# Four layers of a convolutional block on one core: new buffers, two spills to DRAM, and layers 1 to 3 as passes over small blocks

## The chip, the core and the metric

The kernel runs on one core of one Trainium2 chip. The core has a matrix engine (TensorE, PE in the profile, with its weight loads shown apart as PEld), three engines that work element by element (VectorE or DVE, ScalarE or ACT, GpSimd or POOL), and SyncE (SP), which here only issues DMA transfers. Each engine runs its own list of instructions in order, and they wait for each other through semaphores. Data sits in SBUF, 128 partitions wide; matmuls write to PSUM, whose banks hold 512 f32 values per partition. The metric is the device time of one execution in microseconds; the kernel before takes 4568.75 us as the median of three runs (4568.31 to 4569.31).

## The reference

The input x has 4 images of 256 channels and 64 x 64 positions, N = 4096 positions in all, in f32. Each of four layers computes `x = x + layer(gn(x))`, where `gn` is a group norm over groups of 8 channels.

- Layer 0: a 3x3 convolution of 256 to 256 channels, a group norm (groups of 32) and relu give `xs`. Three 1x1 projections of `xs` to 128 channels give theta, phi and g. `softmax(theta^T phi) g` over all 4096 x 4096 pairs gives y. A 1x1 convolution back to 256 channels, a second group norm, and `w_y * 0.1 + xs` is the layer's result.
- Layer 1: each position's channels are scaled to unit length; a 384x256 matrix gives q, k and v in 4 heads of 32. q is softmaxed over the 32 channels of a head, k over the 4096 positions. `context = k v^T` per head, `out = context^T q`, a 256x128 matrix, and again unit length.
- Layer 2: two small networks (256 to 8 channels, relu, mean over positions) make, for each image, a 3x3 kernel for each channel and a 256x256 matrix. The layer is the depthwise 3x3 convolution and then that matrix.
- Layer 3: the channel means go through a small network and a softmax over 4 experts; the layer is a product with the mixed 256x256 matrix.

## The kernel before

Channels lie on partitions in two halves `h` of 128, positions along the free dimension. `forward` (L33) holds the whole state in a pool of 8 buffers of 128x4096 f32, called slots: the residual `r`, normalised copies (`xn`, `xg`), `xs`, theta, phi, g, the attention's probabilities, q, k, v and qT of layer 1, `dw` of layer 2, and streamed weights (`wp2`, `ex`). For every image it calls `layer0` to `layer3` one after the other.

- `group_stats` (L124) runs `bn_stats` (L130) over 16 pieces of 512 of a finished tensor, joins them (L131), averages over a group with two tiny matmuls against a block matrix (`pm` L133, `pv` L141), and takes a square root on ScalarE (L144) and a reciprocal on VectorE (L145). `normalised` (L160) then writes a whole normalised copy on VectorE (L166).
- In `layer0` the convolution is 18 matmuls (9 taps, 2 channel halves) per 512 output positions into a PSUM tile of 1024 (L286), evicted by ScalarE (L289). Edge rows and columns are cut off by `window`.
- `attention` (L184) takes 512 queries at a time, and runs over 16 blocks `m` of 256 keys: `logits(m+1)` is two matmuls (L196) and one exp of 128x1024 on ScalarE (L198); then two matmuls add to `py` (L206), and VectorE adds the probabilities into `tot` (L211). At the end of the 512 queries, two matmuls of ones with `tot` give the sums `pss` (L214); VectorE takes a reciprocal (L216), two reductions for a range check (L218, L219), and the product with `py`, which overwrites theta (L220). GpSimd adds xs to r meanwhile (L324).
- In `layer1` squares (L359), their sums over channels (`ps_ss` L362, single-column matmuls), qkv (L374), the q softmax with its maximum (L392 to L398), the k maximum over all positions (L408 to L418), the exp of k (L423), the context (L427), the sums of k (L431) and the output loop (L445 to L461) are passes over the whole image.
- In `layer2` the depthwise convolution is done by VectorE in two halves of 32 rows, 9 operations each per channel half (L504, L506), then the 256x256 product (L519) with its residual add (L522).
- In `layer3` the product (L561), the add (L564) and the output DMA, issued by GpSimd (L565).

No order is written out by hand. The program is given to Tile, a planner that puts the instructions of each engine in order when the program is built: of the instructions that are ready by its own estimate of durations, an engine takes the one that stands earliest in the program. It also hands out the buffers of each pool (a tag with a number of buffers) and inserts the waits. So an instruction can stand ahead of others that precede it in the program text, and the engine then keeps to that order whatever the real durations are. The trace shows such cases: statistics of the next image's x stand between the depthwise operations of this one.

After the last image the sums of the softmax are checked against a range; outside it the whole program is run again in another form that subtracts row maxima (`attention_by_rows`). With these inputs it isn't run.

Of the kernel before, what the change touches and what calls it, by code (L numbers as in the profile page):

```python
# [8 lines left out]
F32 = mybir.dt.float32  # L9
# [4 lines left out]
P = 128  # L14
# [11 lines left out]
SUM_MAX, SUM_MIN = 1e30, 1e-25  # L26
# [6 lines left out]
def forward(ctx: ExitStack, tc: tile.TileContext, sums, x, wc, wtpg, ww, wqkv, wout, w1cat, wd2,  # L33
                       bd2, wp2, bp2, experts, rw1, rw2, vec, btp, bg, bo, b1cat, out):

# [6 lines left out]
    slots = ctx.enter_context(tc.tile_pool(name="slots", bufs=9 if sums is None else 8))  # L42
# [6 lines left out]
    def slot(name):  # L49
        return slots.tile([P, N], F32, tag="slot", name=name)  # L50
# [7 lines left out]
    def acc(name):  # L58
        return psa.tile([P, 512], F32, tag="acc", name=name)
# [123 lines left out]

    def attention(b, theta, phi, g):  # L184

        NM = N // CH * 4
        for q in range(NQ):
            cols = bass.ts(q, 512)
            py = acc("ps_y")
            tot = tp.tile([P, CH], F32, tag="tot", name="tot")  # L190
            probs = slot(f"pr_{b}_{q}").rearrange("p (k n) -> p k n", n=CH)

            def logits(m):
                ps = wide("ps_f")
                for s in range(2):
                    nc.tensor.matmul(ps[:, bass.ts(s, 512)], phi[:, bass.ts(2 * m + s, P)], theta[:, cols],  # L196
                                     start=True, stop=True)
                nc.scalar.activation(probs[:, m % 4, :], ps, AF.Exp)  # L198

            logits(0)  # L200
            for m in range(NM):
                if m + 1 < NM:
                    logits(m + 1)
                pr = probs[:, m % 4, :]
                for s in range(2):
                    nc.tensor.matmul(py, g[:, bass.ts(2 * m + s, P)], pr[:, bass.ts(s, 512)],  # L206
                                     start=(m == 0 and s == 0), stop=(m == NM - 1 and s == 1))
                if m == 0:
                    nc.vector.tensor_copy(tot, pr)
                else:  # L210
                    nc.vector.tensor_tensor(tot, tot, pr, ALU.add)  # L211
            pss = bank("ps_sum")
            for s in range(2):
                nc.tensor.matmul(pss, ones, tot[:, bass.ts(s, 512)], start=(s == 0), stop=(s == 1))  # L214
            inv = tp.tile([P, 512], F32, tag="inv", name="inv", bufs=1)
            nc.vector.reciprocal(inv, pss)  # L216
            at = b * NQ + q
            nc.vector.tensor_reduce(sums[:, 0, at:at + 1], pss, AX.X, ALU.max)  # L218
            nc.vector.tensor_reduce(sums[:, 1, at:at + 1], pss, AX.X, ALU.min)  # L219
            nc.vector.tensor_tensor(theta[:, cols], py, inv, ALU.mult)  # L220

    def attention_by_rows(b, theta, phi, g):
# [48 lines left out]
    def layer0(b, r):  # L271
# [54 lines left out]
        if sums is None:  # L326
            attention_by_rows(b, theta, phi, g)
        else:
            attention(b, theta, phi, g)
# [247 lines left out]
def conv_preact_kernel(ctx: ExitStack, tc: tile.TileContext, *args):  # L577
# [3 lines left out]
    sums = gp.tile([P, 2, B * NQ], F32, name="sums")  # L581
    forward(tc, sums, *args)

    ext = gp.tile([P, 2], F32, name="ext")
    nc.vector.tensor_reduce(ext[:, 0:1], sums[:, 0, :], AX.X, ALU.max)
    nc.vector.tensor_reduce(ext[:, 1:2], sums[:, 1, :], AX.X, ALU.min)
    nc.vector.tensor_scalar(ext[:, 0:1], ext[:, 0:1], SUM_MAX, None, ALU.is_le)
# [4 lines left out]
    with tc.If(in_range < 1):  # L594
        forward(tc, None, *args)
# [58 lines left out]
```

## Time and profile before

| | |
|---|---|
| median of 3 runs | 4568.75 us (4568.31 to 4569.31) |
| the profiled execution: its own time, its span | 4574.75 us, 4573.0 us |
| mean granted TensorE clock | 0.905 |
| TensorE busy | 3885.9 us, 85% of the span |
| VectorE busy | 1932.7 us, 42% |
| ScalarE busy | 934.0 us, 20% |
| GpSimd busy | 92.4 us, 2% |
| DMA | 51.90 MB, 11 GB/s over the span |

The span runs from the first instruction to the last. A row of a group of instructions gives the line, the engine, the operation, the tiles written and read, the shape and the count, then busy time and mean duration. TensorE's records need care: one f32 matmul is two records, a busy TensorE isn't TensorE at its peak, and its clock is granted in steps that the profile shows (1.00 is full). Idle time of an engine that isn't the bound costs nothing.

### The profile page before, as it was taken

To read this page: it belongs to the slowest core of one execution; us is meant where nothing else is said; L and a number is where in the kernel's file an instruction comes from. 1 tells how busy PE (TensorE), PEld (TensorE's weight loads), DVE (VectorE), ACT (ScalarE), POOL (GpSimd) and SP (SyncE) were. 2 spreads that over 40 slices of the span, in tenths; PEclk is the share of its full clock that TensorE was granted. 3 is DMA by queue.
4 is the path that set the end of the run, shared out by engine and by line. 5 is a ranking of instruction groups with operands and counts; after the bars stand their busy time and mean duration, and the time that the engine had idled before them with its cause. 6 is when DMAs were issued, how large, how long until landed. Compare 5 with 4: busy or idle time off the path is not lost.

```text
span 4573.0 us, 25690 instructions
## 1 busy us (share of the span) xinstructions
PE 3885.9 (85%) x10388; PEld 1917.5 (42%) x10388; DVE 1932.7 (42%) x2154; ACT 934.0 (20%) x1324; POOL 92.4 (2%) x71
## 2 busy tenths in 40 slices
PE   8999998764999999875499999987459999997845
PEld 3444443541444444353244444435324444443622
DVE  1014444569101444556810244454781024445477
ACT  0022223220002222322000222232100022223210
POOL 0010000000001000000000100000000010000000
PEclk9999999676999999967799999997779999998777
DMA  1000000000000000000100000000010000000000
GB/s 72 0 0 0 1 0 0 19 19 34 30 0 0 0 0 0 0 19 19 44 21 0 0 0 1 0 0 19 19 53 12 0 0 0 0 0 0 19 9 38
DMA packets 10318, 51.90 MB, mean 11 GB/s; under 512 B 1744, under 2 KB 2512, under 8 KB 6992
## 3 DMA queue, kind: packets, MB, share of 16 engines
q1 hardware_dynamic: 5584, 33.41, 2.0%
q0 software_dynamic: 4608, 16.78, 0.9%
q8 instruction: 83, 1.36, 0.1%
q14 instruction: 43, 0.35, 0.0%
HBM read 33.40 MB, written 16.78 MB: 11 GB/s over the span
## 4 chain that ended last, share of the span: by engine, by line
PE 66%; issue 19%; DVE 13%; ACT 1%; DMA 0%; POOL 0%; SPq 0%; POOLq 0%; ACTq 0%; DVEq 0%
PE ps_conv L286 21%; PE ps_f L196 14%; PE ps_y L206 14%; DVE dw L506 5%; PE ps_qkv L374 3%; DVE st L130 2%; PE ps_tp L305 2%; PE ps_ex L561 2%; PE ps_ss L362 2%; PE ps_h L474 1%; PE ps_g L315 1%; PE ps_wy L337 1%; PE ps_sum L214 1%; PE ps_pw L519 1%; DVE z L455 1%
## 5 line engine op out<-in xcount | busy, mean ns | idle before, releaser
L211 DVE TENSOR_TENSOR tot<-tot,pr 128x1024 f32<-128x1024 f32 x480 | 588.3, 1226 | 959.5 <-ACT pr L198 956.3
L286 PE MATMUL ps_conv<-xn,wc_s 128*128 128x504 f32 (+3 forms) x2304 | 978.0, 588 | 9.1 <-DVE xn L166 9.1
L196 PE MATMUL ps_f<-theta,phi 128*128 128x512 f32 x2048 | 957.1, 592 | 0.0
L206 PE MATMUL ps_y<-pr,g 128*128 128x512 f32 x2048 | 957.1, 592 | 0.0
L198 ACT ACTIVATE pr<-ps_f 128x1024 f32<-128x1024 f32 x512 | 524.3, 1024 | 1290.4 <-PE ps_f L196 1290.4
L286 PEld LDWEIGHTS ps_conv<-xn,wc_s 128*128 128x128 f32 x2304 | 440.2, 191 | 544.4 <-issue 538.3
L206 PEld LDWEIGHTS ps_y<-pr,g 128*128 128x128 f32 x2048 | 389.1, 190 | 489.8 <-issue 474.2
L196 PEld LDWEIGHTS ps_f<-theta,phi 128*128 128x128 f32 x2048 | 388.8, 190 | 487.9 <-issue 486.0
L130 DVE BATCH_NORM_STATS2 st<-xs 128x6 f32<-128x512 f32 x64 | 41.2, 685 | 930.3 <-ACT xs L289 930.3
L519 PE MATMUL ps_pw<-dw,pk 128*128 128x512 f32 x256 | 131.1, 671 | 265.7 <-DVE pk L512 208.0
L506 DVE SCALAR_TENSOR_TENSOR dw<-xn,dk,dw 128x2016 f32<-128x2016 f32 (+3 forms) x128 | 286.4, 2295 | 0.0
L289 ACT ACTIVATE xs<-ps_conv,vec_s 128x1024 f32<-128x1024 f32 x32 | 35.6, 1114 | 954.3 <-PE ps_conv L286 954.3
L374 PE MATMUL ps_qkv<-wqkv_s,xg 128*128 128x384 f32 x512 | 204.1, 557 | 18.1 <-DVE k L378 9.5
L519 PEld LDWEIGHTS ps_pw<-dw,pk 128*128 128x128 f32 x256 | 54.0, 217 | 339.9 <-DVE pk L512 208.4
L130 DVE BATCH_NORM_STATS2 st<-x 128x6 f32<-128x512 f32 x256 | 160.9, 675 | 5.9 <-DMA x<-in_x_dram 5.7
L216 DVE RECIPROCAL inv<-ps_sum 128x512 f32<-128x512 f32 x32 | 107.4, 3357 | 91.8 <-PE ps_sum L214 91.8
L133 PE MATMUL pm<-mv,avg 128*128 128x2 f32 x48 | 12.2, 323 | 156.9 <-DVE mv L131 156.9
L144 ACT ACTIVATE rstd<-rstd 128x2 f32<-128x2 f32 x24 | 4.9, 204 | 684.7 <-DVE rstd L143 684.7
L561 PE MATMUL ps_ex<-xn,wm 128*128 128x512 f32 x256 | 117.7, 623 | 30.6 <-DVE wm L553 30.6
L374 PEld LDWEIGHTS ps_qkv<-wqkv_s,xg 128*128 128x128 f32 x512 | 106.2, 216 | 85.2 <-issue 18.7
L305 PE MATMUL ps_tp<-xs,wtpg_s 128*128 128x512 f32 x256 | 123.1, 637 | 10.4 <-ACT xs L296 10.4
L362 PEld LDWEIGHTS ps_ss<-ones,sq 128*128 128x128 f32 x512 | 108.3, 313 | 16.0 <-issue 11.2
(145 smaller groups left out, 2316.1 us busy)
## 6 DMA issues: line engine op xcount, KB each, us to landing
x<-in_x_dram SPq DMA_DIRECT2D x16, 1024.0 KB, 7.0
out_dram<-x POOLq DMA_DIRECT2D x32, 512.0 KB, 2.9
wp<-in_wp_dram SPq DMA_DIRECT2D x4, 2048.0 KB, 7.7
ex<-in_experts_dram SPq DMA_DIRECT2D x4, 1024.0 KB, 4.7
wc_s<-in_wc_dram SPq DMA_DIRECT2D x1, 2304.0 KB, 15.9
wtpg_s<-in_wtpg_dram SPq DMA_DIRECT2D x1, 384.0 KB, 15.9
wqkv_s<-in_wqkv_dram SPq DMA_DIRECT2D x1, 384.0 KB, 13.1
bp_s<-in_bp_dram SPq DMA_DIRECT2D x1, 256.0 KB, 2.8
```

The costliest lines, as they stand in the source:

```text
L130: nc.vector.bn_stats(st[:, h, c, :], src[h][:, bass.ts(c, 512)])
L196: nc.tensor.matmul(ps[:, bass.ts(s, 512)], phi[:, bass.ts(2 * m + s, P)], theta[:, cols], start=True, stop=True)
L198: nc.scalar.activation(probs[:, m % 4, :], ps, AF.Exp)
L206: nc.tensor.matmul(py, g[:, bass.ts(2 * m + s, P)], pr[:, bass.ts(s, 512)], start=(m == 0 and s == 0), stop=(m == NM - 1 and s == 1))
L211: nc.vector.tensor_tensor(tot, tot, pr, ALU.add)
L286: nc.tensor.matmul(dst[:, oy, ox], wc_s[:, h, 3 * ty + tx, bass.ts(oh, P)], image(xn[h])[:, iy, ix], start=(k == 0), stop=(k == 17))
L305: nc.tensor.matmul(ps[:, bass.ts(s, 512)], wtpg_s[:, h, k, :], xs[h][:, bass.ts(2 * c + s, 512)], start=(h == 0), stop=(h == NH - 1))
L362: nc.tensor.matmul(pss[:, 4 * c + j:4 * c + j + 1], sq[:, h, bass.ts(j, P)], ones[:, 0:1], start=(h == 0), stop=(h == NH - 1))
L374: nc.tensor.matmul(ps[:, s, 0:3 * HID], xg[h][:, bass.ts(2 * j2 + s, P)], wqkv_s[:, h, :], start=(h == 0), stop=(h == NH - 1))
L506: nc.vector.scalar_tensor_tensor(dst[:, oy, ox], src, dk[:, t:t + 1], dst[:, oy, ox], ALU.mult, ALU.add)
L519: nc.tensor.matmul(ps[:, bass.ts(s, 512)], pk[:, h, bass.ts(oh, P)], dw[h][:, bass.ts(2 * c + s, 512)], start=(h == 0), stop=(h == NH - 1))
L561: nc.tensor.matmul(ps[:, bass.ts(s, 512)], wm[:, h, bass.ts(oh, P)], xg[h][:, bass.ts(2 * c + s, 512)], start=(h == 0), stop=(h == NH - 1))
```

## The change

`forward` is replaced by `conv_preact_fast`; the old form lives on only as the fallback behind the range check (`conv_preact_general`). The new one does the following.

- Fixed buffers instead of slots: `xp` holds the normalised input with a row of zeros above and below each channel half, `big` (128 x 2 x 4096) holds the convolution's output and later the residual stream, `tpg` holds theta, phi and g. Working tiles are small: seven of 128x1024 (`k4`), five of 128x512 (`k2`). PSUM: three banks under one tag (`bank`), three `pf` for the logits, two `acc` for `py` and the sums.
- x is normalised in place, one channel half on VectorE, the other on ScalarE. The convolution writes one bank per 512 positions, with statistics taken right after each eviction.
- After norm and relu, `xs` is written to DRAM (`xs_d`). The attention's result is written to DRAM per 512 queries (`y_d`). Both are read back in `nonlocal_out`, with x itself, which is loaded a second time.
- In attention, exp runs on pieces of 512, three `pr` buffers replace a slot, the two halves of `tot` are added by VectorE before one sum matmul, and the range check's second value comes from a ScalarE pass over the reciprocal (`junk`).
- The statistics that the next norm needs are taken inside the pass that makes the data. The norms are not applied as separate copies in front of layers 2's small network and layer 3's product, but folded into the weights (`w1n`, `wm`, with `b1n`, `b3`).
- Layer 1 runs over eight blocks of 512 positions. It takes no maxima in its softmaxes; the sum of k comes from a column of ones beside v (`v1`), accumulated with the context in `pctx`.
- Reciprocal square roots are taken on GpSimd with `pow` instead of a ScalarE square root and a VectorE reciprocal.
- The depthwise convolution runs in four pieces of 16 rows, its centre tap on ScalarE.
- All output is issued by SyncE.

```diff
+    def k4(name):
+        return wk.tile([P, CH], F32, tag="k4", name=name, bufs=7)
+    def k2(name):
+        return wk.tile([P, 512], F32, tag="k2", name=name, bufs=5)
+    def bank(name):
+        return pp.tile([P, 512], F32, tag="bank", name=name, bufs=3)
+    xp = cp.tile([P, NH, HW + 2, HW], F32, name="xp")
+    big = cp.tile([P, NH, N], F32, name="big")
+    tpg = cp.tile([P, 3, N], F32, name="tpg")
...
+    def rsqrt(o, v):
+        nc.gpsimd.tensor_tensor(o, v, half[:, 0:v.shape[1]], ALU.pow)
...
+    def attend(b):
...
+            def logits(m):
+                pr = wk.tile([P, CH], F32, tag="pr", name="pr", bufs=3)
+                for s in range(2):
+                    pf = pp.tile([P, 512], F32, tag="pf", name="pf", bufs=3)
+                    nc.tensor.matmul(pf, phi[:, bass.ts(2 * m + s, P)], theta[:, cols], start=True, stop=True)
+                    nc.scalar.activation(pr[:, bass.ts(s, 512)], pf, AF.Exp)
+                probs[m] = pr
...
+            nc.vector.scalar_tensor_tensor(inv, tot[:, 0:512], 1.0, tot[:, 512:CH], ALU.mult, ALU.add,
+                                           accum_out=guard[:, 0, at:at + 1])
+            pss = pp.tile([P, 512], F32, tag="acc", name="pss", bufs=2)
+            nc.tensor.matmul(pss, ones, inv, start=True, stop=True)
+            nc.vector.reciprocal(inv, pss)
+            junk = k2("junk")
+            nc.scalar.activation(junk, inv, AF.Copy, accum_out=guard[:, 1, at:at + 1])
+            yt = k2("yt")
+            tt(yt, py, inv, ALU.mult)
+            nc.sync.dma_start(out=y_d[b, :, cols], in_=yt)
+    def nonlocal_out(b):
...
+        for c in range(N // CH):
+            cols = bass.ts(c, CH)
+            for h in range(NH):
+                xs, xr = k4("xs"), k4("xr")
+                nc.sync.dma_start(out=xs, in_=xs_d[b, h, :, cols])
+                nc.sync.dma_start(out=xr, in_=x[b, bass.ts(h, P), cols])
+                stt(xs, big[:, h, cols], sc[:, h:h + 1], xs, ALU.mult, ALU.add)
+                stt(big[:, h, cols], xs, sh[:, h:h + 1], xr, ALU.add, ALU.add)
+                for s in range(2):
+                    nc.vector.bn_stats(st[:, h, 2 * c + s, :], big[:, h, bass.ts(2 * c + s, 512)])
...
+    def linear_attention(b, st):
...
+        pctx = bank("ps_ctx")
+        for c in range(N // 512):
...
+            sq = k4("sq").rearrange("p (h n) -> p h n", h=NH)
+            nc.scalar.activation(sq, xg, AF.Square)
+            s2 = k2("s2")
+            tt(s2, sq[:, 0, :], sq[:, 1, :], ALU.add)
+            ps = bank("ps_ss")
+            for j in range(4):
+                nc.tensor.matmul(ps[:, j:j + 1], s2[:, bass.ts(j, P)], ones[:, 0:1], start=True, stop=True)
...
+            rsqrt(rinv, rinv)
...
+            for j in range(4):
+                ps = bank("ps_qkv")
...
+                nc.scalar.activation(qk[:, j, :], ps[:, 0:2 * HID], AF.Exp, scale=rinv[:, j:j + 1])
+                nc.scalar.activation(v1[:, j, 0:P], ps[:, 2 * HID:3 * HID], AF.Copy, scale=rinv[:, j:j + 1])
...
+            pt = bank("ps_qt")
...
+            for j in range(4):
+                nc.tensor.matmul(pctx[:, 0:P + 1], qk[:, j, HID:2 * HID], v1[:, j, :],
+                                 start=(c == 0 and j == 0), stop=(c == N // 512 - 1 and j == 3))
...
+    def generated(b, st):
...
+        for j in range(R):
+            w = k2("wp2")
+            nc.sync.dma_start(out=w, in_=wp2[:, j, :])
+            stt(pk, w, pb[:, R + j:R + j + 1], pk, ALU.mult, ALU.add)
...
+    def tail(b):
+        mixed(b, generated(b, linear_attention(b, nonlocal_out(b))))
+    for b in range(B):
+        if b > 0:
+            load_x(b)
+        convolve(b)
+        project()
+        attend(b)
+        tail(b)
```

## The prediction

> **What bounds the kernel now.** I read the page first: its busy line, then the slices, then the chain.
>
> ```profile
> span 4573.0 us, 25690 instructions
> PE 3885.9 (85%) x10388; PEld 1917.5 (42%) x10388; DVE 1932.7 (42%) x2154; ACT 934.0 (20%) x1324; POOL 92.4 (2%) x71
> PE   8999998764999999875499999987459999997845
> PEclk9999999676999999967799999997779999998777
> ```
>
> The four images are four equal periods. TensorE is full for two thirds of each and thin in the last third, where the granted clock falls as well. So I cut the second image into its stages with busy times by stretch (columns: PE, PEld, DVE, ACT, POOL, each with its count, then granted clock, DMA share and GB/s):
>
> ```profile
> 1165.00:1409.00 244.00, 243.76 (x576) 110.00 (x576) 13.24 (x19) 7.80 (x7) 0.00 (x0) 0.99 0.00 0
> 1409.00:1416.00 7.00, 1.01 (x5) 0.59 (x4) 3.11 (x12) 2.22 (x3) 0.00 (x0) 0.88 0.00 0
> 1416.00:1461.00 45.00, 44.61 (x193) 27.69 (x194) 9.00 (x8) 13.88 (x13) 18.56 (x8) 0.94 0.00 0
> 1461.00:1914.00 453.00, 453.00 (x1057) 200.63 (x1056) 188.66 (x157) 131.07 (x128) 0.00 (x0) 1.00 0.00 0
> 1914.00:1961.00 47.00, 18.01 (x45) 9.06 (x44) 40.83 (x68) 20.93 (x21) 0.00 (x0) 0.67 0.00 0
> 1961.00:2076.00 115.00, 97.66 (x418) 74.67 (x419) 47.32 (x67) 31.98 (x64) 0.00 (x0) 0.74 0.05 19
> 2076.00:2129.00 53.00, 28.53 (x133) 22.01 (x133) 43.99 (x74) 16.11 (x74) 0.00 (x0) 0.85 0.11 40
> 2129.00:2150.00 21.00, 16.95 (x34) 3.50 (x33) 6.46 (x13) 6.17 (x16) 0.00 (x0) 0.83 0.00 1
> 2150.00:2267.00 117.00, 34.74 (x74) 15.29 (x74) 116.77 (x106) 3.12 (x5) 0.00 (x0) 0.65 0.07 27
> 2267.00:2301.00 34.00, 30.13 (x68) 13.54 (x68) 12.76 (x18) 0.20 (x1) 4.30 (x8) 0.94 0.30 124
> ```
>
> These are: convolution; its norm; projections; attention; output projection with two norms; layer 1 up to its context; layer 1's output; layer 2's hidden layer; depthwise, pointwise and layer 3's gate; layer 3's product. Convolution, projections and attention are TensorE-bound at full clock, 742 of 1136 us. The other third is bound by VectorE (depthwise) or by serial steps on small pieces. Only there can a rewrite of layers 1 to 3 gain.
>
> **The change, per image.** Matmul counts below are pairs of records: one f32 matmul of 512 columns is two records of 0.43 us, 0.86 us.
>
> *Convolution, +2.5 us.* Border rows are now zero rows that are multiplied. The edge forms (441 and 448 columns, 192 records over four images) become 504 and 512: 3040 more columns per image at 512 in 0.43 us. Evictions of 512 on ScalarE and statistics on VectorE lie under 7.7 us of matmul each (uncovered, 16 x 1.25 = 20 us). The norm after it loses a 1.12 us eviction of 1024 for 0.6, one of two last statistics (0.65), sqrt and reciprocal (0.2 each), and gains a `pow` on GpSimd and three small VectorE steps: 0.
>
> **The unknown p.** No row has that `pow` on 128x2 or 128x4. POOL's nearest rows are a 128x128 select, 0.29 us, and a 128x1024 two-operand operation, 2.35 us. The size is nearest the first, the operation heavier, so I take p = 1.0 and keep 0.3 to 2.4. It cannot be below nothing, but the 0.4 us of sqrt and reciprocal it replaces are counted as gone. About eight lie on each image's path.
>
> *Attention, -6.9 us.* The two sum matmuls become one, after a VectorE add of the halves: 0.86 us less, eight times. By the timeline of a query block's end:
>
> ```profile
> 429.28 1.22 DVE L211 TENSOR_TENSOR tot<-tot,pr 128x1024 f32<-128x1024 f32 x1 [2.21 <-ACT pr L198]
> 431.45 1.88 PE L214 MATMUL ps_sum<-tot,ones 128*128 128x512 f32 x4
> 433.17 3.60 PE L196 MATMUL ps_f<-theta,phi 128*128 128x512 f32 x8
> 433.37 3.36 DVE L216 RECIPROCAL inv<-ps_sum 128x512 f32<-128x512 f32 x1 [2.87 <-PE ps_sum L214]
> ```
>
> The last add ends 0.9 us before the sum starts, so the new 0.75 us add still fits. The next block's logits cover the reciprocal: two pairs take 3.44 us, then the first `py` needs an accumulator bank, freed by the reciprocal 3.4 us after the sum. That is the new edge; three `pr` buffers let a third pair run. Exp in halves costs ScalarE 2 x 0.6 us per 3.44 us. Uncovered, the danger is ScalarE's queue (first rival).
>
> *Output projection to layer 1, +7.* After the last sum: 16 matmuls 13.75 us. They cover the last y trip: reciprocal 3.36, product 0.68, write and read about 2.9 each (the nearest rows are 512 KB written in 2.9 and 256 KB read in 2.8), under 11 us in all. Then eviction 0.6, statistics 0.65, group norm 3.6 with p, shift and affine 1.2: 5.8. Then VectorE alone: 8 x (two scalar_tensor_tensor of 1024 at 1.25, by 512 in 0.75 and 2016 in 2.3; two statistics at 0.61) = 29.8. Then group norm 3.6, ScalarE's first normalisation 0.6, hand-overs 0.6. Sum 54 for 47. Before, ScalarE shared the add, GpSimd had added x under attention, and statistics cost 16 x 0.61.
> The 16 reloads of 512 KB sit under those 29.8 if two land per 3.7 us. These rows give 2.9 us for 512 KB and 1.5 MB more in 4.8, so 3.2 us for two; seven buffers are filled during attention.
>
> ```profile
> out_dram<-x POOLq DMA_DIRECT2D x32, 512.0 KB, 2.9
> wp<-in_wp_dram SPq DMA_DIRECT2D x4, 2048.0 KB, 7.7
> ```
>
> The Trainium skill ("DMA: Bandwidth & Descriptors", section Bandwidth) speaks against this: batch to at least 1 MiB, about 2 us being fixed per transfer. Taken as serial, its fit would price 16 loads at some 51 us and this stage 20 us dearer; I go by the rows, since the transfers overlap.
>
> *Layer 1 to its context, -25.* Before, normalise, squares, sums, qkv, two softmaxes, context and key sums follow each other; 7.0 us is one k maximum, and 256 single-column sum records run at clock 0.50. The change drops both maxima, halves the sums, folds key sums into context, and runs eight blocks. In one block TensorE has sums 1.4, eight matmuls of 384 columns 5.4 (0.34 a record), four transposes 0.5, context 1.2: 8.5 us. ScalarE has 2 x 0.62 + 1.06 + 4 x (0.42 + 0.36) + 0.6 = 6.0, VectorE 2.5. `pctx` holds one of three banks; on two, a block's end is exp, sum 0.66, reciprocal 0.25, product 0.68, transposes, copy 0.6, while the next block's sums use the other. That leaves TensorE some 0.9 us idle: 9.4 us, or 9.9 at clock 0.95. First block 9.3, seven more 69, drain and w2 6: 84 for 115; I take 90 for unevenness, with 85 to 130.
>
> *Layer 1's output, 0.* VectorE per block: 2 x 0.68 + 0.15 + 1.22 + 2 x (0.74 + 0.61) = 5.4, so 44, plus 8 to start: 52 for 53. Statistics move in here from layer 2.
>
> *Layers 2 and 3, -3.5.* The hidden layer loses the normalisation ahead of it, but ScalarE now has 8 x 0.87 + 8 x 1.23 = 16.8 us: 19.8 for 21.5 with the centre tap. Depthwise: 64 operations of 1.18 (75.5; before 32 of 2.21 and four centres), pk 5.3, pointwise adds 16 x 0.70, statistics 16 x 0.61, less 1.3 of pk in a wait: 100.5. Last pointwise 3.2, group norm 3.6, gate and mix 6.7: 114 for 117. Layer 3's 29 us stay; pm of the next image can have a bank only after ps_ex: 5.7 us for 4.6.
>
> *DMA issue, 0.* SyncE issues 73 transfers per image for 6: 4 of x, 8 of xs, 16 of y, 16 reloads, 9 of layer 2's weights in pieces, 4 of the experts, 16 of output; GpSimd issues none of the output's 8. At 0.33 to 0.5 us an issue that is some 30 us of its queue, spread over 1136. The next x is issued when depthwise has left its buffer, some 19 us ahead of layer 3's product, and lands (7.0 us for 1 MB, four at once) under the gate and that product's 29 us; if not, up to 11 us more per image. Weight pieces come through five buffers, under depthwise.
>
> Sum: 2.5 - 6.9 + 7 - 25 + 0 - 3.5 = -26 per image, -104. The profiled execution took 4574.75 us (span 4573.0 and 1.75 around it), 6.0 above the median of 4568.75. So 4471 on its scale, **4466** as a median.
>
> On layer 1 the clock matters most. Its row: granted 0.74 there now, 0.50 under single-column sums though TensorE shows busy. The Trainium skill ("TensorE: Matmul & The Clock Gate", Part 1) says half rate comes after an idle window of about 3.4 us. By that rule a block with 0.9 us of idle would stay warm, at 9.4; if 1.4 us sums counted as idle, still no window is empty.
>
> **Rivals.**
> 1. *ScalarE's queue blocks at each query block's end.* `junk` reads the reciprocal. If it stands ahead of the next block's exps, these start 3.4 + 0.6 us after the sum; three `pf` banks hold 2.6 us of logits: 2.25 us stall, 32 times, +72: 4538. For: the planner writes the order by its own estimates, and it put a 7.08 us reduction between two steps of the q softmax. Against: TensorE has no gap at any of 32 ends before.
> 2. *Layer 1's blocks do not overlap* (slower). One block in series: 1.24 + 1.06 + 0.7 + 1.4 + 0.2 + p + 4.7 evictions + 1.7 softmax + 0.5 + 0.6 + hand-overs 0.5 = 13.6, at clock 0.74 about 15.6: 125 + 9 for my 90, +44 per image: 4642. For: `bank` is shared with `pctx`, and buffers seem given out in program order (the next image's loads waited for layer 1's end). Against: before, qkv already ran between the sums. It decides from 90 + 26 = 116 us, so from 9.9 + 26/8 = 13.1 us a block.
> 3. *`pow` is slow* (slower). Beyond the rows, p = 5 costs 8 x 4 = 32 per image: 4594. It decides at 1 + 26/8 = 4.3 us.
> 4. *The spill shows.* If pairs of reloads take 6 us, 48 for 29.8: +18 per image, 4538.
> 5. *The change does little:* gains and losses inside 0.2% (9 us, about what can be told from no change).
>
> ```profile
> 898.16 7.08 DVE L408 TENSOR_REDUCE km<-k 128x128 f32<-128x4096 f32 x1
> 905.15 1.22 DVE L393 TENSOR_TENSOR q<-q,qred 128x1024 f32<-128x1024 f32 x1
> ```
>
> **How the numbers follow.** Forecast 0.42; rivals 0.20, 0.18, 0.08, 0.10; little change 0.02. Low end: layer 1 at 85 and p at 0.3, (5 + 5.6) x 4 = 42 off: 4424. High end takes in rival 2, 4642; a blocked and cold version beyond it is left out. Faster: nearly all of the forecast, three quarters of rivals 1 and 4: 0.63. Slower: rivals 2 and 3, and the ends of 1 and 4: 0.31. Same 0.06. The forecast alone spans 4424 to 4515.
>
> **What would show it.** Attention at about 446 us per image without TensorE gaps; the stretch from last sum to first qkv near 54 with VectorE solid; layer 1's blocks every 9 to 10 us at clock over 0.9; POOL `pow` rows of about 1 us; clock and VectorE of the depthwise stretch as before. I am wrong if the blocks go beyond 13 us, if ScalarE waits for a reciprocal between blocks, or if VectorE waits for reloads.

## The result and the profile after

The changed kernel takes 4725.65 us (median of 4 runs, 4723.11 to 4727.16) against 4569.03 us for the kernel before, measured beside it: a ratio of 1.0342, 95% interval 1.0324 to 1.036. It is 3.4% slower, where the forecast said 2.2% faster; the time lies 84 us above the range's upper end. The profiled execution took 4723.11 us.

The page of the kernel after, its span, busy line of TensorE, and two rows of the 40 slices:

```profile
span 4721.1 us, 26366 instructions
...
PE 3917.5 (83%) x9858; PEld 1887.4 (40%) x9858; DVE 1785.5 (38%) x2202; ACT 1137.2 (24%) x2107; POOL 84.3 (2%) x131
...
PE   7999997745999999675599999967459999996745
...
PEclk9999998767999999876799999977679999997767
```

TensorE has fewer matmul records than before (9858 for 10388) and yet 32 us more busy time: some of the same work ran at a lower clock (granted 0.892 on average, for 0.905 before). The four thin stretches are still there, and they are longer.

The second image cut into the same stages as in the prediction (columns as there: stretch and length, PE, PEld, DVE, ACT, POOL with counts, granted clock, DMA share, GB/s):

```profile
1201.00:1449.00 248.00, 247.53 (x576) 110.33 (x576) 11.92 (x17) 12.03 (x18) 0.00 (x0) 0.99 0.00 0
1449.00:1455.00 6.00, 0.71 (x4) 0.59 (x4) 2.54 (x12) 1.17 (x2) 0.69 (x1) 0.76 0.00 0
1455.00:1500.00 45.00, 43.95 (x193) 27.34 (x194) 4.84 (x7) 18.90 (x24) 0.00 (x0) 0.96 0.48 175
1500.00:1946.00 446.00, 446.00 (x1042) 197.51 (x1041) 181.66 (x151) 156.35 (x270) 0.00 (x0) 1.00 0.01 5
1946.00:2011.00 65.00, 19.28 (x48) 9.54 (x46) 48.11 (x73) 12.46 (x21) 1.45 (x3) 0.64 0.33 106
2011.00:2116.00 105.00, 87.10 (x287) 57.03 (x286) 18.76 (x41) 43.54 (x95) 8.45 (x15) 0.76 0.00 0
2116.00:2199.00 83.00, 41.81 (x137) 33.05 (x138) 44.91 (x73) 14.81 (x66) 8.75 (x9) 0.64 0.00 0
2199.00:2219.00 20.00, 16.21 (x36) 3.43 (x33) 1.49 (x8) 15.63 (x26) 0.00 (x0) 0.90 0.19 55
2219.00:2338.00 119.00, 44.27 (x75) 17.61 (x76) 116.60 (x142) 7.70 (x9) 0.70 (x1) 0.68 0.16 55
2338.00:2375.00 37.00, 33.17 (x76) 15.51 (x76) 14.27 (x26) 1.11 (x1) 0.70 (x1) 0.87 0.29 114
```

Beside the forecast, in us per image (the last column is the run both_bank_edits, told below: the same text with two bank edits):

| stage | before | forecast | after | both_bank_edits |
|---|---|---|---|---|
| convolution, norm, projections | 296 | 298.5 | 299 | 299.3 |
| attention | 453 | 446.1 | 446 | 446.5 |
| last sum to first qkv | 47 | 54 | 65 | 61.2 |
| layer 1, first pass (qkv to ps_o) | 115 | 90 | 105 | 72.3 |
| layer 1, output pass (ps_o to ps_h) | 53 | 52 | 83 | 54.0 |
| hidden layer | 21 | 19.8 | 20 | 20.1 |
| depthwise to gate | 117 | 114 | 119 | 119.3 |
| layer 3's product, next norm | 34 | 34.7 | 37 | 36.9 |

In the kernel before the first qkv stands at 1959.04, two us ahead of the cut that the prediction made; counted from it, 47 and 115 are 45 and 117.

Four images times the differences from the forecast (11 + 15 + 31 + 5 + 2, some 64) are 256 of the 260 us by which the forecast missed. Half of it is in the output pass, which was forecast at no change.

Rows from the timeline of the output pass, weight loads left out (start, length, engine, line, work; in brackets the idle time before and what ended it):

```profile
2124.26 1.97 PE L403 MATMUL ps_zt<-ident,z 128*128 128x128 f32 x8 [4.27 <-DVE z L56]
2126.01 2.86 PE L391 MATMUL ps_o<-w,xp 128*128 128x256 f32 x8
...
2128.12 1.48 DVE L56 TENSOR_TENSOR z<-ps_o,bo_s 128x512 f32<-128x512 f32 x2
2128.89 0.42 ACT L396 ACTIVATE junk<-z 128x256 f32<-128x256 f32 x1 [7.24 <-DVE z L56]
...
2130.89 1.01 POOL L125 TENSOR_TENSOR zr<-zr,half 128x4 f32<-128x4 f32 x1 [7.95 <-DVE zr L397]
2131.93 1.22 DVE L56 TENSOR_TENSOR z<-z,zr 128x1024 f32<-128x1024 f32 x1 [1.12 <-POOL zr L125]
2133.30 1.94 PE L403 MATMUL ps_zt<-ident,z 128*128 128x128 f32 x8 [4.42 <-DVE z L56]
...
2135.03 3.46 PE L391 MATMUL ps_o<-w,xp 128*128 128x256 f32 x8
```

Each block goes through every engine before the next begins: ps_o, add, squares, pow, product, transposes, 9.0 to 9.9 us a block. On TensorE the next block's ps_o stands behind this block's ps_zt, although it needs nothing of it. TensorE idles 4.3 to 4.9 us a block, and the clock goes to 0.64. Before, four blocks of ps_o (32 records) ran ahead of the first transposes, and the pass took 53 us:

```profile
2075.65 9.28 PE L445 MATMUL ps_o<-w,qT 128*128 128x256 f32 x32 [0.58 <-DVE w L440]
2086.38 1.09 PE L459 MATMUL ps_zt<-ident,z 128*128 128x128 f32 x8 [1.45 <-DVE z L455]
```

The first pass of the kernel after, TensorE alone (the last row ends with the window):

```profile
2063.83 8.44 PE L352 MATMUL ps_qkv<-wqkv_s,xg 128*128 128x384 f32 x16 [0.33 <-DVE rinv L343]
2072.11 0.83 PE L368 MATMUL ps_ctx<-v,qk 128*128 128x129 f32 x6
2073.37 0.49 PE L368 MATMUL ps_ctx<-v,qk 128*128 128x129 f32 x2 [0.43 <-ACT v L355]
2075.18 0.63 PE L364 MATMUL ps_qt<-ident,qk 128*128 128x128 f32 x4 [1.31 <-DVE qk L56]
2075.64 0.95 PE L341 MATMUL ps_ss<-ones,s 128*128 128x1 f32 x8
2076.92 3.48 PE L352 MATMUL ps_qkv<-wqkv_s,xg 128*128 128x384 f32 x5 [0.33 <-DVE rinv L343]
```

A block is 12.7 to 13.1 us here, the first one 14.0. The next block's sums and qkv stand behind this block's ps_qt, which waits for the q softmax; the qkv matmuls themselves take 7.0 to 8.4 us (8.4 in the block shown) where the forecast had 5.4.

### The profile page after: what moved, and what is told of

It reads as the page before. It is cut to its first block, busy times and chain, and to the rows that moved or that the text cites. A ratio compares the mean times of both kernels' runs of the same rounds, so it can differ in the third digit from the quotient of the medians.

```text
span 4721.1 us, 26366 instructions
## 1 busy us (share of the span) xinstructions
PE 3917.5 (83%) x9858; PEld 1887.4 (40%) x9858; DVE 1785.5 (38%) x2202; ACT 1137.2 (24%) x2107; POOL 84.3 (2%) x131
## 3 DMA queue, kind: packets, MB, share of 16 engines
q8 instruction: 80, 1.31, 0.1%
## 5 line engine op out<-in xcount | busy, mean ns | idle before, releaser
L231 PE MATMUL ps_conv<-xp,wc_s 128*128 128x504 f32 (+1 forms) x2304 | 990.7, 594 | 10.3 <-DVE xp L203 10.3
L268 PE MATMUL pf<-tpg 128*128 128x512 f32 x2048 | 957.1, 592 | 0.0
L278 PE MATMUL py<-pr,tpg 128*128 128x512 f32 x2048 | 957.1, 592 | 0.0
L269 ACT ACTIVATE pr<-pf 128x512 f32<-128x512 f32 x1024 | 607.9, 596 | 1143.2 <-PE pf L268 1143.2
L231 PEld LDWEIGHTS ps_conv<-xp,wc_s 128*128 128x128 f32 x2304 | 441.6, 192 | 556.4 <-issue 543.7
L278 PEld LDWEIGHTS py<-pr,tpg 128*128 128x128 f32 x2048 | 389.1, 190 | 489.8 <-issue 483.1
L268 PEld LDWEIGHTS pf<-tpg 128*128 128x128 f32 x2048 | 388.8, 190 | 487.9 <-issue 481.2
L59 DVE SCALAR_TENSOR_TENSOR dw<-xp,dk,dw 128x1008 f32<-128x1008 f32 (+1 forms) x256 | 309.6, 1260 | 5.0 <-ACT dw L462 4.9
L246 PE MATMUL ps_tp<-big,wtpg_s 128*128 128x512 f32 x256 | 123.4, 628 | 15.1 <-ACT big L216 12.0
L527 PE MATMUL ps_ex<-big,wm 128*128 128x512 f32 x256 | 124.8, 649 | 0.0
```

The costliest lines, as they stand in the source:

```text
L59: nc.vector.scalar_tensor_tensor(o, a, s, b, op0, op1)
L231: nc.tensor.matmul(dst[:, :, x0:x1], wc_s[:, h, 3 * ty + tx, bass.ts(oh, P)], xp[:, h, c * RB + ty:c * RB + ty + RB, x0 + dx:x1 + dx], sta ...
L246: nc.tensor.matmul(ps, wtpg_s[:, h, k, :], big[:, h, cols], start=(h == 0), stop=(h == NH - 1))
L268: nc.tensor.matmul(pf, phi[:, bass.ts(2 * m + s, P)], theta[:, cols], start=True, stop=True)
L269: nc.scalar.activation(pr[:, bass.ts(s, 512)], pf, AF.Exp)
L527: nc.tensor.matmul(ps[oh], wm[:, h, bass.ts(oh, P)], big[:, h, cols], start=(h == 0), stop=(h == NH - 1))
```

## The experiments

**Theory.** The planner gives a tag's buffers out in the order of the program text, when it places the instruction that first writes them. ps_o of block c+1 and ps_zt of block c share the tag `bank`; ps_zt comes first in the text, so ps_o of the next block gets no bank until this block's last stage has been placed, though a bank stands free. In the first pass ps_ss and ps_qkv of block c+1 wait for ps_qt of block c in the same way. **Rivals:** three banks are too few whatever the order; the cold clock stretches a chain that would otherwise fit; and, for the stretch after attention, y's trip through DRAM.

**1. own_banks_out.** ps_o moves to the three `pf` banks, which are idle after attention (`pf_bank` and `acc_bank` are helpers that take a tile of the tag `pf` or `acc`).

```
-                ps = bank("ps_o").rearrange("p (j o) -> p j o", j=2)
+                ps = pf_bank("ps_o").rearrange("p (j o) -> p j o", j=2)
```

> Edit: the changed kernel, with layer 1's output pass taking its ps_o tiles from the three pf banks, which are idle there, instead of from the bank tag that ps_zt uses as well. No work is added or left out. Theory B (banks): a tag's banks are handed out in the order of the program's first uses, so ps_o of the next block can't get one until ps_zt of this block is placed, and the blocks run one after the other (9.5 us a block, 83 us for the pass). With its own banks the pass is bound by VectorE's 5.4 us a block: about 55 us, 27 us less per image, 4725 - 108 = 4617. Theory W (work): the pass is slow for what was put into it, statistics 1.28 and pow with its hand-overs 1.3 us a block, and for the half clock of its matmuls; then it stays within 3 us of 83, and the time within 4713 to 4738.

Measured: 4615.19 us, ratio to before 1.0098 (1.0081 to 1.0115), 110.5 us less than the kernel after. The output pass by windows (columns as above, here and in what follows):

```profile
2089.20:2143.90 54.70, 32.52 (x137) 25.76 (x138) 42.28 (x73) 14.28 (x65) 8.75 (x9) 0.72 0.00 1
```

From 82.7 to 54.7 us, as expected. VectorE, which the forecast had as the bound, is now busy for 42 of 55 us. This changes both the order of hand-out and the number of banks; experiments 5 and 6 part the two.

**2. own_banks_ctx.** ps_ss goes to the `acc` banks, ps_qt and the context to `pf`; qkv keeps the three of `bank`.

```
-        pctx = bank("ps_ctx")
+        pctx = pf_bank("ps_ctx")
...
-            ps = bank("ps_ss")
+            ps = acc_bank("ps_ss")
...
-            pt = bank("ps_qt")
+            pt = pf_bank("ps_qt")
```

> Edit: the changed kernel, with layer 1's first pass taking ps_ss from the two acc banks and ps_qt and pctx from the three pf banks; ps_qkv keeps the bank tag. No work is added or left out. Theory B: the blocks run every 12.9 us now since ps_ss of the next block must wait for ps_qt of this one, which stands behind the q softmax; TensorE thins out to clock 0.77. With own banks qkv of the next block fills that time: 9.5 to 10 us a block, clock over 0.9, 105 us become about 82, 23 us less per image, 4725 - 92 = 4633. Theory W: ScalarE's order (normalisation, squares and exps of two blocks in one queue) or the pow holds the blocks; then under 5 us per image, 4705 or more.

Measured: 4575.73 us, ratio 1.0013 (1.0004 to 1.0023), 149.9 less than after. The first pass by windows:

```profile
1972.70:2044.80 72.10, 65.16 (x291) 42.10 (x291) 20.00 (x42) 44.40 (x96) 8.43 (x15) 0.97 0.00 1
```

72.1 us for 104.7, ten better than expected: TensorE is busy for 65 of 72 us, with 0.7 us of idle time left in a block of 8.4, and the clock is 0.97 where it was 0.76. The stretch ahead of it fell too, from 65.2 to 61.3, since the first qkv no longer stands behind ps_ss; with it the two stretches together went from 169.9 to 133.4. The forecast's 9.9 us a block was too dear; the cost of sharing was larger than the measured 105 against 90 had made it look.

**3. y_in_sbuf.** y overwrites theta, which the query block no longer needs, and never goes to DRAM.

```
-            yt = k2("yt")
-            tt(yt, py, inv, ALU.mult)
-            nc.sync.dma_start(out=y_d[b, :, cols], in_=yt)
+            tt(theta[:, cols], py, inv, ALU.mult)
...
-            yt = k2("yt")
-            nc.sync.dma_start(out=yt, in_=y_d[b, :, cols])
...
-                nc.tensor.matmul(ps, ww_s[:, bass.ts(h, P)], yt, start=True, stop=True)
+                nc.tensor.matmul(ps, ww_s[:, bass.ts(h, P)], theta[:, cols], start=True, stop=True)
```

> Edit: the changed kernel without the spill of y: the attention's result overwrites theta, as before the change, and the output projection reads it there. Theory S (spill on the path): all but one of the eight reads of y stand behind the last write of y in SyncE's queue, and that write waits for the last reciprocal; TensorE waits 5.9 us and starts the rest late. Without the spill the output projection follows the last sum without a gap: 6 to 8 us less per image, 4725 - 28 = 4697. Rival: the wait only moves, since the last piece needs the reciprocal anyway, and the group norm's end is set by it: under 2 us per image, 4717 or more.

Measured: 4682.63 us, ratio 1.0245 (1.0228 to 1.0262), 43.0 less than after: 8.1 us of it per image in the stretch from the last sum to the first qkv (57.1 for 65.2), the rest in the passes behind it. What it removed, in the timeline of the kernel after (SPq is SyncE's list of DMA issues; the last row ends with the window):

```profile
1946.33 1.88 PE L306 MATMUL ps_wy<-yt,ww_s 128*128 128x512 f32 x4
...
1949.92 0.69 DVE L56 TENSOR_TENSOR yt<-py,inv 128x512 f32<-128x512 f32 x1
...
1950.64 0.32 SPq L294 DMA_DIRECT2D y_d<-yt  x1
1951.12 8.60 SPq L303 DMA_DIRECT2D yt<-y_d  x7
...
1954.13 6.10 PE L306 MATMUL ps_wy<-yt,ww_s 128*128 128x512 f32 x10 [5.93 <-DMA yt<-y_d]
```

Seven of the eight reads are issued behind the last write, although six of them fetch pieces that were written long before. So only one pair of matmuls could start at once, and 5.93 us of TensorE were lost. Why the planner put the six there was not tried.

**4. before_shared_banks.** The other way round: the kernel before, with its ps_zt taken from the tag that ps_o uses.

```
-                pt = bank("ps_zt")
+                pt = wide("ps_zt")[:, 0:512]
```

> Edit: the kernel before, with ps_zt of layer 1's output loop taken from the wide tag that ps_o uses, two buffers for both. No work is added or left out, no pow, no statistics in the loop. Theory B: the same hand-out in program order now serialises the blocks here too: from 5.1 to about 9 us a block, 53 us become 75 to 85, 4569 + 4 x 25 = 4669 (4655 to 4700). Theory W: the loop stays at 53 us within 4, since its work is what it was: 4553 to 4585.

Measured: 4719.1 us, ratio 1.0327 (1.031 to 1.0344). The one line costs the kernel before 150 us, nearly as much as the whole change did. Its output pass by windows:

```profile
2107.90:2198.30 90.40, 43.44 (x133) 32.77 (x134) 47.63 (x74) 16.76 (x74) 0.00 (x0) 0.65 0.06 23
```

90.4 us where before had 53.2, clock 0.65 for 0.85; 37.2 x 4 is the 150 us. The expectation was right in kind and a third too small (150 us more than before, for 100; the time is above its band of 4655 to 4700). Two buffers now serve both stages, so this run alone doesn't part order from number; 5 and 6 do.

**5. one_ring_six_banks.** The text unchanged; `bank` and `pf` become one tag of six.

```
-        return pp.tile([P, 512], F32, tag="bank", name=name, bufs=3)
+        return pp.tile([P, 512], F32, tag="bank", name=name, bufs=6)
...
-                    pf = pp.tile([P, 512], F32, tag="pf", name="pf", bufs=3)
+                    pf = bank("pf")
```

> The kernel after with the pf tag dissolved: all tiles of the bank and pf tags take turns in one ring of six banks, text and order of the program as they are. If banks are too few, six instead of three free the next block: the output pass falls to 55 us or less, the first pass of layer 1 below 90 too, the time to 4615 or below. If it is the order in which a tag's banks are handed out (a bank for the next block's ps_o isn't given before this block's ps_zt has its own), six banks change nothing there: the output pass stays at 80 to 85 us an image, the whole at 4710 to 4735.

Measured: 4704.52 us (4699.48 to 4712.57), ratio 1.029 (1.0274 to 1.0305). The first pass and the output pass by windows:

```profile
2011.20:2112.40 101.20, 85.47 (x285) 55.47 (x285) 18.75 (x41) 43.70 (x95) 8.43 (x15) 0.77 0.00 0
2112.40:2195.20 82.80, 41.70 (x135) 32.94 (x135) 44.95 (x73) 14.61 (x65) 8.74 (x9) 0.66 0.00 0
```

Twice the banks change the output pass by nothing (82.8 for 82.7) and the first pass by 3.5 us. It is not their number. (The time came out 5 us below the expected band.)

**6. front_written_first.** Three shared banks as in the kernel after; only the text is turned, so that ps_o and the adds of the next block stand ahead of this block's squares and transposes.

```
-        for c in range(N // 512):
-            cols = bass.ts(c, 512)
+        def front(c):
             z = k4("z").rearrange("p (j o) -> p j o", j=4)
...
+            return z
+
+        zn = front(0)
+        for c in range(N // 512):
+            cols = bass.ts(c, 512)
+            z = zn
+            if c + 1 < N // 512:
+                zn = front(c + 1)
             zr = sp.tile([P, 4], F32, name="zr", bufs=3)
```

> The kernel after with its three shared banks, but the output loop written so that the ps_o matmuls and the adds of bo of block c+1 stand ahead of the squares and transposes of block c. No bank is added. If the order of hand-out is the cause, the blocks overlap again: output pass 54 to 58 us instead of 83, the whole at 4610 to 4630, as with banks of its own. If three banks are too few for the overlap, it stays above 70 us and 4680.

Measured: 4629.04 us, ratio 1.0128 (1.0112 to 1.0143). The output pass by windows:

```profile
2095.40:2152.90 57.50, 35.47 (x137) 28.37 (x138) 42.23 (x73) 14.11 (x65) 8.75 (x9) 0.71 0.00 1
```

57.5 us without one bank more. With 5, this settles the output pass: the order of hand-out, not the number. It could not be the planner's preference for earlier text alone either, since in experiment 1 the text was as in the kernel after and only the tag differed. That a buffer is given out at its first write, and not at another point, is part of the theory that no run tried.

**7. warm_fill.** Two 128x512 matmuls more a block, into a bank that nobody reads, in TensorE's idle time.

```
+            for s in range(2):
+                wm = pp.tile([P, 512], F32, tag="pf", name="wm", bufs=3)
+                nc.tensor.matmul(wm, ident, z.rearrange("p j o -> p (j o)")[:, bass.ts(s, 512)], start=True, stop=True)
             zr = sp.tile([P, 4], F32, name="zr", bufs=3)
```

> The kernel after with two matmuls of 128x512 more a block in the output pass, which read z after the adds, write a pf bank that nobody reads, and fall into the 4.4 us in which TensorE waits for z. They prolong no other engine's work. If a cold clock is a good part of the 83 us, the granted clock of this window rises from 0.64 to 0.8 or more, the block's own matmuls (3.6 + 1.9 + 1.9 us cold) shrink by a quarter or more, and the pass falls to 70 to 76 us, the whole to 4690 to 4705. If the serial chain through VectorE, ScalarE and GpSimd is all of it, the pass stays at 82 to 86 us and the whole at 4720 to 4740.

Measured: 4699.56 us, ratio 1.0282 (1.0266 to 1.0298), 26 us less with more work done. The output pass by windows, and the groups of its matmuls (count, then busy us and mean ns of one record):

```profile
2113.70:2189.60 75.90, 48.42 (x167) 31.10 (x168) 43.91 (x73) 14.26 (x65) 8.75 (x9) 0.84 0.00 1
```

```profile
L391 PE MATMUL ps_o<-w,xp 128*128 128x256 f32 x256 | 85.5, 494 | 1.9 <-ACT w L382 1.9
...
L395 PE MATMUL wm<-z,ident 128*128 128x512 f32 x128 | 66.6, 644 | 13.9 <-DVE z L56 13.6
...
L406 PE MATMUL ps_zt<-ident,z 128*128 128x128 f32 x256 | 43.2, 323 | 76.4 <-DVE z L56 76.4
```

In the kernel after these records took 584 and 423 ns. The clock rose from 0.64 to 0.84 and the pass fell by 6.8 us, of the 28 that the overlap gives. So the lower clock is about a quarter of the loss, as far as this filling removes it. The overlapped passes of 1 and 6 take 54.7 and 57.5 us at a clock of only 0.71 to 0.72: it is the overlap that makes them short, not the clock.

**8. both_bank_edits.** Experiments 1 and 2 together, y still through DRAM.

```
-        pctx = bank("ps_ctx")
+        pctx = pf_bank("ps_ctx")
...
-            ps = bank("ps_ss")
+            ps = acc_bank("ps_ss")
...
-            pt = bank("ps_qt")
+            pt = pf_bank("ps_qt")
...
-                ps = bank("ps_o").rearrange("p (j o) -> p j o", j=2)
+                ps = pf_bank("ps_o").rearrange("p (j o) -> p j o", j=2)
```

> The change as made, y through DRAM as it is, with the two bank edits only (ps_o in the pf banks; ps_ss, ps_qt and ps_ctx in acc and pf banks). If the hand-out of banks is the one step of the forecast that failed, what is left is the forecast: 4725.65 less 110.5 and 149.9 is 4465, with the 13.6 us by which the three edits together fell short of their sum 4479; qkv to ps_o about 72 us, output pass 52 to 55. If something else took a good part of the difference, it stays above 4510.

Measured: 4461.46 us (4460.4 to 4464.07), ratio 0.9765 (0.9751 to 0.9778). Where the forecast had 4466. Its stages are the table's last column; the two passes of layer 1 by windows:

```profile
1947.00:2019.30 72.30, 65.29 (x292) 42.15 (x292) 20.00 (x42) 44.53 (x97) 8.45 (x15) 0.97 0.00 1
2019.30:2073.30 54.00, 31.44 (x137) 24.90 (x138) 42.30 (x73) 14.76 (x66) 8.76 (x9) 0.72 0.00 1
```

In sum the change does gain what was forecast; the assignment of banks took 264 us, more than all of it.

**9. all_three_mended.** The four lines of both_bank_edits and y over theta.

```
-                ps = bank("ps_o").rearrange("p (j o) -> p j o", j=2)
+                ps = pf_bank("ps_o").rearrange("p (j o) -> p j o", j=2)
...
-            tt(yt, py, inv, ALU.mult)
-            nc.sync.dma_start(out=y_d[b, :, cols], in_=yt)
+            tt(theta[:, cols], py, inv, ALU.mult)
```

> All three edits in one kernel: the output pass's ps_o in the pf banks, ps_ss, ps_qt and ps_ctx in acc and pf banks, y written over theta instead of to DRAM. If the three costs are separate, their gains add: 4725.65 less 110.5, 149.9 and 43.0 is 4422, a period of image 1 of about 1099, and faster than the kernel before by about 3 %. If they share a cost (one and the same cold clock, or the shortage of banks that only moves on), the gains overlap and the time stays between 4450 and 4530.

Measured: 4435.63 us (4435.19 to 4435.94), ratio 0.9705 (0.9692 to 0.9718): the fastest kernel of this study. The two bank edits add up (264.2 for 260.4 as a sum). The time lies between the two bands of the expectation (4422, and 4450 to 4530). y kept in SBUF adds 25.8 here and not 43.0: the stretch after the last sum falls by 8.0 us an image as it did alone (61.2 to 53.2), some 32 in all. Alone, the two passes behind it gained another 10 us over the four images; here they lost 2 (the first pass takes 73.2 us on average for 72.7). (The two profiled executions differ by 28.2 us, the medians by 25.8.) In the kernel after these passes ran at a clock of 0.76 and 0.64; that this is the reason was not tried by itself.

**10. both_passes_by_order.** No more banks; beside 6, the first pass takes normalisation, squares and sums of the next block ahead of this block's qkv and softmax.

```
-        for c in range(N // 512):
+        def front(c):
...
             rsqrt(rinv, rinv)
+            return xg, rinv

+        nxt = front(0)
+        for c in range(N // 512):
+            cols = bass.ts(c, 512)
+            xg, rinv = nxt
+            if c + 1 < N // 512:
+                nxt = front(c + 1)
             qk = k4("qk").rearrange("p (j o) -> p j o", j=4)
```

> No bank more than in the kernel after; the text of both passes of layer 1 is put in another order: the output loop as in front_written_first, and in the first pass the normalisation, squares and ps_ss of block c+1 ahead of the qkv, softmax and ps_qt of block c. Order theory: in the first pass the next block's sums and their pow no longer lie behind this block's transposes, so a block takes 9.5 to 10.5 us and not 12.9, the pass 80 to 88 us, the whole 4629 less 4 x (17 to 25): 4530 to 4561. If the first pass is short of banks (pctx holds one of three), it stays at 100 us or more and the whole at 4610 to 4630.

Measured: 4602.29 us, ratio 1.0073 (1.0058 to 1.0088), a miss: the first pass went from 104.7 to 99.4 us only, while the stretch ahead of it grew by 2.7. The run falls into neither band of the expectation (its second one, for a lack of banks, began at 100 us and 4610), but is next to the second. The pass by windows:

```profile
1985.30:2084.70 99.40, 82.15 (x276) 53.36 (x276) 18.01 (x39) 41.48 (x92) 7.42 (x14) 0.79 0.00 0
```

But in this text ps_qt of block c still stands ahead of ps_qkv of block c+1, so TensorE still has nothing to do during the softmax. The last two runs part that from the number of banks.

**11. softmax_written_last.** As 10, with the front carried on through qkv: the q softmax, ps_qt and ps_ctx of block c stand behind qkv of block c+1. Three banks.

```
-        for c in range(N // 512):
+        def front(c):
...
                 nc.scalar.activation(v1[:, j, 0:P], ps[:, 2 * HID:3 * HID], AF.Copy, scale=rinv[:, j:j + 1])
+            return qk, v1

+        nxt = front(0)
+        for c in range(N // 512):
+            cols = bass.ts(c, 512)
+            qk, v1 = nxt
+            if c + 1 < N // 512:
+                nxt = front(c + 1)
             q = qk[:, :, 0:HID].rearrange("p j (g d) -> p j g d", d=HD)
```

> Three shared banks as in the kernel after; both loops in another order of text. In the first pass the q softmax, ps_qt and ps_ctx of block c now stand behind everything up to the qkv matmuls of block c+1, so that qkv need not wait for a bank that this block's ps_qt gets first. Order theory: TensorE has qkv of c+1 to do during the softmax of c; a block takes 9 to 10.5 us instead of 12.9, the pass 78 to 88 us, the whole 4529 to 4570. If two free banks are too few whatever the order, the pass stays at 95 us or more and the whole at 4590 or above.

Measured: 4479.3 us (4478.78 to 4480.98), ratio 0.9803 (0.9787 to 0.982). The first pass by windows, and TensorE's timeline in it:

```profile
1954.30:2023.10 68.80, 64.67 (x285) 43.40 (x285) 18.18 (x41) 42.36 (x95) 8.65 (x15) 0.95 0.00 1
```

```profile
1981.29 5.33 PE L352 MATMUL ps_qkv<-wqkv_s,xg 128*128 128x384 f32 x16
1986.45 0.60 PE L371 MATMUL ps_qt<-ident,qk 128*128 128x128 f32 x4
1986.89 1.06 PE L375 MATMUL ps_ctx<-v,qk 128*128 128x129 f32 x8
1988.05 1.02 PE L341 MATMUL ps_ss<-ones,s 128*128 128x1 f32 x8
1988.93 0.47 PE L375 MATMUL ps_ctx<-v,qk 128*128 128x129 f32 x2
1989.23 5.33 PE L352 MATMUL ps_qkv<-wqkv_s,xg 128*128 128x384 f32 x16
```

68.8 us, nine better than the expected band. With banks of their own (experiment 2) it was 72.1, but there the first qkv ran ahead of ps_ss and the count began 4 us earlier; with the stretch ahead the two come to 133.9 and 133.4 us, the same. A block is 7.9 us with no idle time on TensorE, and qkv is back at the forecast's 5.4. The same three banks, two of them free, suffice.

**12. softmax_last_six_banks.** The text of 11 with the one tag of six banks of 5.

```
-        return pp.tile([P, 512], F32, tag="bank", name=name, bufs=3)
+        return pp.tile([P, 512], F32, tag="bank", name=name, bufs=6)
```

> softmax_written_last with one ring of six banks in place of three and three. Order theory alone: no more than 3 us an image below softmax_written_last in the first pass. If order and number of banks are both needed there, the pass falls to 70 to 78 us here, as with banks of its own, and stays 8 us or more above that in softmax_written_last; the whole to 4490 to 4520.

Measured: 4464.23 us, ratio 0.9772 (0.9756 to 0.9788); the first pass 67.9 us. Six banks are worth 0.9 us there. Order alone explains nearly all of both passes of layer 1: from the kernel after to experiment 11 the text order moved 246 us, where banks of their own moved 264. The 15 us between 11 and 12 are, per image, that 0.9, 1.6 in the output pass (56.5 to 54.9) and 1.1 in the projections (44.7 to 43.6). 11 was not tried with y in SBUF.

## Why the prediction was wrong, by its own steps

**Layer 1's output, 0: the step that failed.** It divided VectorE's work by blocks (5.4 us each) and added a start of 8, which holds only if blocks overlap. VectorE's work was about right (44.9 us), the overlap was not there: 83 us for 52. That the tags are shared was seen, and that buffers seem to be given out in program order too, but both were asked of the first pass alone. The output loop takes ps_o and ps_zt from the same `bank`, where the kernel before had two tags; the prediction's term for this loop does not mention it. Made with overlap, the pass takes 54.0 to 57.5 us: the term itself was good.

**Layer 1 to its context, -25.** Measured -10 (105 for 115); with the banks mended -43 (72.3) and by order -46 (68.8, counted from a later start). The step was wrong twice, in opposite directions. It let the sums of the next block run during the softmax, which the sharing forbade; the holes came to 2.1 us in the block shown, for the 0.9 that it had, and at the lower clock qkv took 7.0 to 8.4 us for 5.4. And where blocks do overlap it was too dear: a block takes 7.9 to 8.4 us for 9.9, the sums 1.0 for 1.4, with part of the context beside them, and the 6 us for unevenness did not show.

**Rival 2** (blocks don't overlap, 4642) had the mechanism, in one place of two, and a chance of 0.18. In that place the blocks took 12.7 to 13.1 us, at most the 13.1 from which it was to decide, and the pass 105 of its 116. Its price was 44 us an image; it cost 15 here and 31 in the pass that it did not look at, and that the two add up to about its price is luck.

**Output projection to layer 1, +7.** Measured +18 in the kernel after. VectorE's part was right: adds and statistics from 1973.8 to 2002.4, 28.6 us for 29.8, without waits for reloads, so rival 4 did not occur. The reloads took longer than the 2.9 us of the rows that the prediction went by (medians of 6.7 and 7.6 us from issue to landing over the whole run), but lay under VectorE's work all the same; the 51 us of the prediction's serial price did not come true either. Wrong was "they cover the last y trip": it priced the last piece and took the seven others to be there, while the reads stood behind the last write (8.1 us, experiment 3). Another 4 us were the first qkv behind ps_ss (experiment 2). Without both the stretch takes 53.2 us, as forecast.

**Attention, -6.9:** 446 for 446.1, with no TensorE gap between query blocks; rival 1 did not occur. **Convolution, +2.5:** 248 for 246.5.

**The unknown p:** 0.70 us on 128x2 and 1.01 us on 128x4 for the 1.0 taken; rival 3 did not occur. The groups of the kernel after:

```profile
L125 POOL TENSOR_TENSOR zr<-zr,half 128x4 f32<-128x4 f32 x32 | 32.2, 1007 | 310.6 <-DVE zr L397 310.6
L125 POOL TENSOR_TENSOR rstd<-rstd,half 128x2 f32<-128x2 f32 x24 | 16.7, 698 | 3927.2 <-DVE rstd L166 3927.2
```

**Layers 2 and 3, -3.5:** measured +4. The hidden layer was right (20 for 19.8). For the depthwise stretch the sum counted 16 statistics and forgot the 16 of the next image's x, 10.4 us of VectorE there; VectorE is busy 116.6 of 119 us, and the stretch takes 5 us more than forecast, so the rest of the sum was some 5 us too dear. Layer 3's product and the next norm take 37 for 34.7.

That both_bank_edits landed 5 us from 4466 is in part luck: against the forecast it has -18 us an image in the first pass, and +7, +2, +5 and +2 elsewhere.

**Slips in the sums.** The 5.8 us in the output projection's term are 6.05 by their own parts, and the last step gives 4465 for 4466; neither moves the forecast. Rival 1's stall of 2.25 us is not what its terms leave (4.0 less 2.6). The single-column sums of the kernel before are 192 records an image, not 256.

**The clock.** The prediction weighed the Trainium skill ("TensorE: Matmul & The Clock Gate", Part 1): half rate after an idle window of about 3.4 us. The output pass agrees (idle 4.3 to 4.9 us a block, clock 0.64; filled, 0.84). For the first pass that rule is not enough: no idle time that the rows of a block above show is longer than 1.31 us, and it was granted 0.76. Idle time is not all that lowers the clock: in the kernel before, single-column sums kept TensorE busy for the whole of 1979.95 to 1993.50, and the clock granted there was 0.50. In the first pass holes, a few transposes and such sums follow one another from 2072.94 to 2076.92. Which of them lowered the clock, no run parts; with the same sums and few or no holes (experiments 2 and 11) it was 0.95 to 0.97.

## What to carry to other kernels

Where two stages of a loop take PSUM from one tag, read the loop in text order: the next block's first tile comes after this block's last one, and twice the buffers did not change that here. Give the stages tags of their own, or write the loop so that the next block's front stands ahead of this block's back. When a rewrite saves buffers, sum each pass twice, once by its busiest engine and once as one block in series, and find in the text what lets the blocks overlap before taking the smaller sum.

## What the runs showed that was not expected

Extra matmuls made the kernel faster: 128 records of 128x512 in idle time (66.6 us of TensorE) saved 26 us; the blocks ran in the same order, and the clock in that pass rose from 0.64 to 0.84. The Trainium skill ("Perfetto Trace Analysis", section Matmuls) says that independent matmul groups should rotate through different PSUM banks so that the eviction of one overlaps the matmuls of the next; the kernel after does so over three banks, and with six (experiment 5) its output pass was as long, 82.8 us. Rotation is not sufficient; the order in which the turns are taken decides.
